# Turning the experts' activations: TensorE transposes replaced by a VectorE block transpose and ScalarE copies

## The chip, the core and the metric

The kernel runs on one core of a Trainium2 chip. A core has five engines that run in parallel, each through its own instructions in order: TensorE (PE, matrix products into PSUM), VectorE (DVE), ScalarE (ACT), GpSimd (POOL) and SyncE (SP). They wait for each other through semaphores. Data lie in SBUF, 128 partitions, and come from and go to device memory by DMA. The metric is the time of one execution on the device, in microseconds; lower is better.

## The reference

A layer norm feeds two branches whose results are added to the input: a gated linear recurrence with an output projection (`Wo`), and a mixture of 64 experts. The change is in the experts. Each takes up to 128 tokens of width 1024 and has a hidden width of 384:

```python
h = jax.nn.silu(jnp.einsum('ecd,efd->ecf', xg, w1)) * jnp.einsum('ecd,efd->ecf', xg, v1)
y = jnp.einsum('ecf,efd->ecd', h, w2)
yr = y[e_s, pos_c] * jnp.where(valid, w_s, 0.0)[:, None]
return jnp.zeros((T, D), x.dtype).at[tok_s].add(yr)
```

For the product with `w2`, TensorE sums over partitions, so the hidden features must lie on partitions. They come out of the first product with the tokens on partitions. So `h`, 128 tokens x 384 features, is turned once for each expert into three blocks of 128 features x 128 tokens. How this turn is made is what changes.

## The kernel before

Everything is fp32. The first part (attention, norm, routing, to about 1235 us in the profile) is not touched. The second part, `Experts.run`, treats the experts in a plan of groups: experts 0 and 1 alone, then 31 pairs (2, 3), (4, 5) and so on. Between the experts' products it places *steps* of the output projection of the other branch: 16 units of seven steps each, a step being four 128x512 matmuls of `steps` (L144, 8 rows in the profile, since each fp32 matmul makes two).

The order is written out by hand: inside `in_order`, TensorE, VectorE and ScalarE each keep the order of the program, so an instruction that waits holds all behind it on its engine. For a pair (e, e+1):

1. `hidden(e)` and `hidden(e+1)`: seven half products each (a Strassen-like scheme) into PSUM banks A, B, C, D (`hA` to `hD`), L977. ScalarE copies from the banks (L994 to L1001, L1007) and applies Silu (L1010). VectorE adds (L997 to L1009), turns the next expert's gathered tokens in blocks of 32x32 (`turned`, L920), and multiplies the two halves (L1012). `hidden(e)` also makes sums of the next expert's weights on VectorE (`right_sum`, L959; number 4, t4, is used by the last four matmuls of `hidden(e+1)`).
2. `turn_hidden(e)`: three TensorE transposes into bank D (L1021) and one ScalarE copy to `hT` (L1022).
3. One step of `project`, then `output(e)`: six matmuls with `w2` into banks D and T (L1030), each half scaled into `ys` by ScalarE (L1033), and a scatter with addition into the output from the POOL queue (L1034). There are two `ys` buffers, one for even and one for odd experts. VectorE makes sums for the next pair meanwhile.
4. `turn_hidden(e+1)`, two steps of `project`, `output(e+1)`; in every second pair one more step.

POOL's queue also holds the gathers of tokens (L871) and of token weights (L882), and the writes of the projection into the output (L1063); writes to the output follow each other. SP's queue holds the loads of the weights (L859) and of the projection's input (L1051).

Of the kernel before, what the change touches and what calls it, by code (L numbers as in the profile page):

```python
# [16 lines left out]
P = 128  # L17
B, S, D = 4, 1024, 1024
# [3 lines left out]
SH = S // 2  # L22
NM = SH // P
E, K, F, C = 64, 8, 384, 128
KF = F // P
TH = P // 2
Q = 32
NQ = P // Q
# [802 lines left out]
class Experts:  # L831
# [57 lines left out]
    def places(self):  # L889


        pools = self.pools
        t = pools.left.tile([P, NSLOT, KH, P], F32, tag="w", name="t23")
        t = t.rearrange("p a b c -> p (a b c)")
        u = pools.block("t4").rearrange("p a b -> p (a b)")
        n = KH * F
        self.t2, self.t3, self.t4 = (
            v.rearrange("p (k f) -> p k f", f=F) for v in (t[:, 0:n], t[:, n : 2 * n], u[:, 0:n])
        )
        self.p6, self.q = t[:, 2 * n : 2 * n + F], u[:, n : n + F]  # L900
        self.hT = self.p6.rearrange("p (j i) -> p j i", i=P)
        self.s = {0: pools.one.tile([P, 4, KH, TH], F32, tag="cur", name="s")}

    def more_places(self):
# [53 lines left out]
        }[n]  # L958
        self.nc.vector.tensor_tensor(to, a, b, ALU.subtract)  # L959

    def hidden(self, e, turn, then_next):

        nc = self.nc
        a11, a12, _, a22 = self.left_blocks(e)
        b11, b21, t1, b22 = self.right_blocks(e)
        s1, s2, s3, s4 = (self.s[e % 2][:, i] for i in range(4))
        ba, bb, bc, bd = (self.banks[n][:, 0:F] for n in "ABCD")  # L970
        lo, hi = slice(0, TH), slice(TH, P)

        def both(left, right):

            for k in range(len(left[3])):
                for half, (bank, a, b, ks) in ((lo, left), (hi, right)):
                    nc.tensor.matmul(  # L977
                        bank[half],
                        lhsT=a[:, ks[k], :],
                        rhs=b[:, ks[k], :],  # L980
                        start=(k == 0),
                        stop=(k == len(ks) - 1),
                        tile_position=(0, half.start),
                    )

        every, q, r, s, up = range(KH), self.q, self.acts[e % 2], self.p6, self.up
        both((bc, s3, self.t3, every), (bc, s4, b22, every))
        if then_next:  # L990
            for n in (3, 1):
                self.right_sum(e + 1, n)
        both((ba, a11, b11, every), (ba, s1, t1, every))
        nc.scalar.copy(q, ba)  # L994
        nc.scalar.copy(r[lo], ba[hi])
        nc.scalar.copy(r[hi], ba[lo])
        nc.vector.tensor_tensor(q, bc, q, ALU.add)  # L997
        nc.vector.tensor_tensor(up, q, r, ALU.add)
        both((bd, s2, self.t2, every), (bb, a12, b21, every))
        nc.scalar.copy(s[hi], bd[lo])  # L1000
        nc.scalar.copy(s[lo], bd[lo])  # L1001
        nc.vector.tensor_tensor(up, up, s, ALU.add)
        nc.vector.tensor_tensor(q[lo], q[lo], s[lo], ALU.add)
        if then_next:
            self.right_sum(e + 1, 2)
        both((bb, a22, self.t4, (0, 1)), (ba, a22, self.t4, (2, 3)))
        nc.scalar.copy(r[lo], ba[hi])  # L1007
        nc.vector.tensor_tensor(r, bb, r, ALU.add)
        nc.vector.tensor_tensor(r[lo], r[lo], q[lo], ALU.add)  # L1009
        nc.scalar.activation(r, r, AF.Silu)  # L1010
        self.turned(turn)
        nc.vector.tensor_tensor(r, r, up, ALU.mult)  # L1012
        if then_next:
            self.right_sum(e + 1, 4)
        for n in range(2):
            del self.weights[e, n]

    def turn_hidden(self, e):
        nc, pt = self.nc, self.banks["D"][:, 0:F].rearrange("p (j i) -> p j i", i=P)
        for j in range(KF):  # L1020
            nc.tensor.transpose(pt[:, j, :], self.acts[e % 2][:, j * P : (j + 1) * P], self.ident)  # L1021
        nc.scalar.copy(self.hT, pt)  # L1022

    def output(self, e):
        nc, ys, hT = self.nc, self.ys[e % 2], self.hT
        w2, wt = self.weights.pop((e, 2)), self.wt[:, e % NWT, e : e + 1]
        for h, cols in enumerate((H0, H1)):
            ps = self.banks["DT"[h]]
            for j in range(KF):
                nc.tensor.matmul(  # L1030
                    ps, lhsT=hT[:, j, :], rhs=w2[:, j, cols], start=(j == 0), stop=(j == KF - 1)
                )
            nc.scalar.mul(ys[:, cols], ps, wt)  # L1033
        nc.gpsimd.indirect_dma_start(  # L1034
            out=self.out,
            out_offset=bass.IndirectOffsetOnAxis(ap=self.idx[:, e : e + 1], axis=0),
            in_=ys,
            in_offset=None,
            compute_op=ALU.add,
        )  # L1040
        self.gather_wt(e + NWT)
# [54 lines left out]
    def run(self):  # L1096
        nc, pools, units = self.nc, self.pools, B * NM
        self.banks = {n: pools.bank(tag, [P, SH], f"h{n}") for n, tag in zip("ABCDT", "abcrt")}
        with in_order(self.tc, [mybir.EngineType.SP]):
            self.load(1, 1)  # L1100
            self.load_wo()
            self.load(0, 2)
            gated = self.load_gated(0)
            self.load(1, 0)
        for e in (1, 2):
            self.gather(e)
        wo_sums = right_sums(nc.vector, self.wo_b, lambda n: pools.block(f"wo_{n}"))

        plan = [((0,), 2, (1,), 0), ((1,), 1, (0,), 0)]
        plan += [((e, e + 1), 0, (1, 2), int(e % 4 == 0)) for e in range(2, E - 4, 2)]
        plan += [((e, e + 1), 0, (1, 1), 0) for e in (E - 4, E - 2)]
        todo, u, left = None, 0, 0

        def project(n):
            nonlocal todo, u, left, gated
            for _ in range(n):
                if left == 0:  # L1120
                    todo, left = self.project(u, gated), NSLOT
                next(todo, None)
                left -= 1
                if left == 0:
                    u += 1
                    gated = self.load_gated(u) if u < units else None

        with in_order(self.tc, ORDERED):
            for n in (2, 4):
                self.right_sum(0, n)  # L1130
            for _ in range(3):
                next(wo_sums)
            self.more_places()
            for g, (group, ahead, between, behind) in enumerate(plan):
                new = group[-1] + 1
                after = plan[g + 1][0] if g + 1 < len(plan) else ()
                for i, e in enumerate(group):
                    self.hidden(e, (*after[i : i + 1], E)[0], e != group[-1])
                    self.load(e + 2, 1)
                    if i == 0:  # L1140
                        self.load(e + 2, 0)
                    else:
                        self.load(e, 2)
                    if i == 0:
                        self.gather(new + 2)
                project(ahead)
                if g == 0:
                    for _ in wo_sums:
                        pass
                for i, e in enumerate(group):  # L1150
                    self.turn_hidden(e)
                    project(between[i])
                    if i == 0:
                        if len(after) > len(group):
                            self.turned(new + 1)
                        for n in after:
                            self.left_sums(n)
                        for n in (3, 1):
                            self.right_sum(new, n)
                    self.output(e)  # L1160
                    if i == 0 and len(group) > 1:
                        self.load(new + 1, 0)
                    if i == 0 and len(after) > 1:
                        self.gather(new + 3)
                    if e == group[-1]:
                        self.load(new, 2)
                        for n in (2, 4):
                            self.right_sum(new, n)
                project(behind)
            for _ in todo:  # L1170
                pass
# [48 lines left out]
```

## Time and profile before

| | |
|---|---|
| median of 3 runs | 2563.79 us (2562.29 to 2563.8) |
| the profiled execution | 2563.14 us, span 2561.4 us, granted TensorE clock 0.999 |
| POOL busy | 805.9 us, 31% |
| two stretches of 44 us among the pairs (1809 to 1853, 1853 to 1897 us) | TensorE busy 44.00 and 44.00, VectorE 29.30 and 29.59, ScalarE 12.73 and 10.99, POOL 19.26 and 15.55; DMA 0.94 and 0.91 busy |
| L1021 transposes 128x128 | 192, 273 ns each |
| L1022 copies 128x384 | 64, 475 ns each |
| L920 VectorE transposes 128x1024 | 64, 1229 ns each |

A row of the order of time has the start in us, the duration in us, the engine, the line, the operation, what it writes and reads, the shape, how many instructions are merged in it, and in brackets how long the engine sat idle before it and what ended that. Matmuls are pipelined: a row's duration is longer than the time after which the next one starts, so TensorE's pace is read from starts.

### The profile page before, as it was taken

The page shows a single profiled execution, that of the slowest core. Times are in us where ns is not written, and L with a number is a line of the kernel's source. Part 1 is how long each engine was busy: PE and PEld are TensorE (multiplying, and loading weights), DVE is VectorE, ACT ScalarE, POOL GpSimd, SP SyncE. Part 2 cuts the span into 40 slices and gives each one's busy share as a digit, 9 for nine tenths or more (in the row PEclk, how much of TensorE's full clock was granted, in tenths as well). Part 3 has the DMA queues.
Part 4 walks back from the last instruction along what each step waited for, and adds up shares of the span by engine and source line. Part 5 has one row for each costly group of instructions (what it writes and reads, how often), then busy time and mean ns, then how long its engine had stood idle before and what let it go on. Part 6 is the DMA issues. An engine that isn't in the chain of part 4 may idle for free.

```text
span 2561.4 us, 23153 instructions
## 1 busy us (share of the span) xinstructions
PE 2540.7 (99%) x8449; PEld 1124.8 (44%) x8449; DVE 1706.0 (67%) x2116; ACT 612.7 (24%) x1055; POOL 805.9 (31%) x631
## 2 busy tenths in 40 slices
PE   9999999999999999999999999999999999999998
PEld 5444444444444444444444444444444444444443
DVE  7956659474693747447776767667676767666673
ACT  3212212031111311112222222223232222223232
POOL 0453302101121110232353434344443434344421
PEclk9999999999999999999999999999999999999999
DMA  5755624543344532145898899989998899889995
GB/s 185 259 173 220 197 82 170 177 148 113 132 140 176 176 140 90 58 170 180 288 348 286 308 304 313 310 291 320 297 325 285 317 303 324 295 299 311 304 324 124
DMA packets 122497, 593.24 MB, mean 232 GB/s; under 512 B 15872, under 2 KB 52736, under 8 KB 89360
## 3 DMA queue, kind: packets, MB, share of 16 engines
q1 hardware_dynamic: 81488, 448.03, 47.7%
q0 software_dynamic: 40464, 143.72, 21.0%
q8 instruction: 67, 1.10, 0.2%
q14 instruction: 46, 0.38, 0.0%
q10 hardware_dynamic: 432, 0.01, 0.0%
HBM read 483.67 MB, written 124.81 MB: 238 GB/s over the span
## 4 chain that ended last, share of the span: by engine, by line
PE 90%; DVE 8%; issue 1%; DMA 1%; ACT 0%; SPq 0%; POOL 0%; POOLq 0%; DVEq 0%; ACTq 0%
PE pa_g L144 8%; PE pa_o L144 8%; PE hC L977 7%; PE hA L977 7%; PE hD L1030 6%; PE hT L1030 6%; PE hD L977 6%; PE pa_q L144 6%; PE pa_v L144 5%; PE pc_g L144 4%; PE pc_o L144 4%; PE pc_q L144 3%; PE hB L977 3%; PE pc_v L144 3%; DVE cur L555 2%; PE pb_o L144 2%
## 5 line engine op out<-in xcount | busy, mean ns | idle before, releaser
L871 POOL DMA_INDIRECT xg<-rows,tables x256 | 307.9, 1203 | 303.4 <-DVE xgT L920 234.8
L959 DVE TENSOR_TENSOR t<-w 128x1536 f32<-128x1536 f32 x128 | 224.1, 1751 | 261.9 <-PE hC L977 259.1
L1034 POOL DMA_INDIRECT out_dram<-ys,tables x64 | 132.9, 2077 | 394.6 <-ACT ys L1033 202.2
L144 PE MATMUL pa_g<-xT,w 128*128 128x512 f32 x512 | 230.8, 594 | 0.0
L144 PE MATMUL pa_v<-xT,w 128*128 128x512 f32 x480 | 216.8, 593 | 2.5 <-ACT sc_v L155 2.5
L144 PE MATMUL pa_q<-xT,w 128*128 128x512 f32 x480 | 216.6, 593 | 1.2 <-ACT sc_q L155 1.2
L977 PE MATMUL hC<-t,s 128*64 128x384 f32 x512 | 177.3, 489 | 0.0
L977 PE MATMUL hC<-w,s 128*64 128x384 f32 x512 | 177.3, 489 | 0.0
L1030 PE MATMUL hD<-w,t 128*128 128x512 f32 x384 | 175.3, 592 | 0.6 <-ACT t L1022 0.6
L977 PE MATMUL hA<-w,s 128*64 128x384 f32 x512 | 175.6, 486 | 0.0
L977 PE MATMUL hD<-t,s 128*64 128x384 f32 x512 | 175.6, 486 | 0.0
L977 PE MATMUL hB<-w,xgT 128*64 128x384 f32 x512 | 175.6, 486 | 0.0
L977 PE MATMUL hA<-w,xgT 128*64 128x384 f32 x512 | 175.6, 486 | 0.0
L1030 PE MATMUL hT<-w,t 128*128 128x512 f32 x384 | 175.2, 592 | 0.0
L144 PE MATMUL pa_o<-wo_T,gated 128*128 128x512 f32 x384 | 172.7, 592 | 0.0
L144 PEld LDWEIGHTS pa_g<-xT,w 128*128 128x128 f32 x512 | 96.4, 190 | 122.9 <-issue 122.1
L701 POOL DMA_DIRECT2D gated<-y x64 | 48.1, 757 | 303.0 <-DVE y L696 288.6
L144 PEld LDWEIGHTS pa_q<-xT,w 128*128 128x128 f32 x480 | 90.9, 190 | 116.6 <-issue 112.7
L144 PEld LDWEIGHTS pa_v<-xT,w 128*128 128x128 f32 x480 | 90.2, 190 | 114.8 <-issue 109.6
L144 PE MATMUL pc_v<-xT,w 128*128 128x512 f32 x256 | 115.4, 593 | 2.2 <-ACT sc_v L155 2.2
L144 PE MATMUL pc_q<-xT,w 128*128 128x512 f32 x256 | 115.4, 593 | 2.1 <-ACT sc_q L155 2.1
L144 PE MATMUL pc_g<-xT,w 128*128 128x512 f32 x256 | 115.5, 594 | 0.0
(243 smaller groups left out, 4309.1 us busy)
## 6 DMA issues: line engine op xcount, KB each, us to landing
w<-in_w_dram SPq DMA_DIRECT2D x128, 1536.0 KB, 9.5
w<-in_v_dram SPq DMA_DIRECT2D x64, 1536.0 KB, 8.7
w<-wsum SPq DMA_DIRECT2D x36, 1792.0 KB, 7.5
wsum<-w POOLq DMA_DIRECT2D x12, 1792.0 KB, 6.1
x<-in_x_dram SPq DMA_DIRECT2D x32, 512.0 KB, 9.3
rows<-x POOLq DMA_DIRECT2D x32, 512.0 KB, 4.6
gated<-y POOLq DMA_DIRECT2D x64, 256.0 KB, 4.7
gated<-gated SPq DMA_DIRECT2D x16, 1024.0 KB, 6.5
```

What stands on the lines that cost most here:

```text
L144: nc.tensor.matmul(ps, lhsT=lhs[:, slot, k, :], rhs=blocks[right][:, k, :], start=start and k == 0, stop=stop and k == KH - 1, skip_group_ ...
L555: nc.vector.match_replace(cur, eight, cur, 0.0)
L701: nc.gpsimd.dma_start(out=gated[b, :, :, slot, m, :].rearrange("u p j -> p u j"), in_=yc[:, h * SH : (h + 1) * SH].rearrange("p (u j) -> p ...
L871: nc.gpsimd.indirect_dma_start(out=self.xg[:, e % 2 * NQ + r, :], out_offset=None, in_=self.rows.rearrange("n (q c) -> (n q) c", q=NQ), in ...
L959: self.nc.vector.tensor_tensor(to, a, b, ALU.subtract)
L977: nc.tensor.matmul(bank[half], lhsT=a[:, ks[k], :], rhs=b[:, ks[k], :], start=(k == 0), stop=(k == len(ks) - 1), tile_position=(0, half.st ...
L1030: nc.tensor.matmul(ps, lhsT=hT[:, j, :], rhs=w2[:, j, cols], start=(j == 0), stop=(j == KF - 1))
L1034: nc.gpsimd.indirect_dma_start(out=self.out, out_offset=bass.IndirectOffsetOnAxis(ap=self.idx[:, e : e + 1], axis=0), in_=ys, in_offset=No ...
```

## The change

The TensorE transposes, their copy and the tile `hT` in the place of t2/t3 go. In their place `split_hidden(e)`, at the end of `hidden(e)`, has VectorE turn the activations in blocks of 32x32 into the left half of `ys`; after it every block is turned, but lies on the partitions of its tokens. `turn_hidden(e)` then makes 16 ScalarE copies, each of three blocks (32 partitions x 3 x 32), from partition quarter r to quarter q, into the right half of `ys`, where `output` reads them.

The place of the turn moves too. In a pair the first expert's copies are issued inside the second's `hidden`, after the copies from bank D (L1001); the second's after the first step of `project`. The plan is rewritten so that each pair has one step ahead of the first output and the rest ahead of the second, as before; the single experts have two steps ahead of the output (before: three around the transposes for expert 0, one for expert 1).

```diff
-        self.hT = self.p6.rearrange("p (j i) -> p j i", i=P)
...
-    def hidden(self, e, turn, then_next):
+    def hidden(self, e, turn, then_next, last=None):
...
         nc.scalar.copy(s[hi], bd[lo])
         nc.scalar.copy(s[lo], bd[lo])
+        if last is not None:
+            self.turn_hidden(last)
...
         nc.vector.tensor_tensor(r, r, up, ALU.mult)
+        self.split_hidden(e)
         if then_next:
             self.right_sum(e + 1, 4)
...
+    def split_hidden(self, e):
+
+        t = self.ys[e % 2][:, 0:F]
+        self.nc.vector.transpose(
+            t.rearrange("p (x i) -> p x i", i=Q), self.acts[e % 2].rearrange("p (x j) -> p x j", j=Q)
+        )
+
     def turn_hidden(self, e):
-        nc, pt = self.nc, self.banks["D"][:, 0:F].rearrange("p (j i) -> p j i", i=P)
-        for j in range(KF):
-            nc.tensor.transpose(pt[:, j, :], self.acts[e % 2][:, j * P : (j + 1) * P], self.ident)
-        nc.scalar.copy(self.hT, pt)
+
+        split = self.ys[e % 2][:, 0:F].rearrange("p (j q i) -> p j q i", q=NQ, i=Q)
+        for r in range(NQ):
+            for q in range(NQ):
+                self.nc.scalar.copy(
+                    self.hT(e)[q * Q : (q + 1) * Q, :, r * Q : (r + 1) * Q],
+                    split[r * Q : (r + 1) * Q, :, q, :],
+                )
+
+    def hT(self, e):
+
+        return self.ys[e % 2][:, SH : SH + F].rearrange("p (j i) -> p j i", i=P)
...
-        plan = [((0,), 2, (1,), 0), ((1,), 1, (0,), 0)]
-        plan += [((e, e + 1), 0, (1, 2), int(e % 4 == 0)) for e in range(2, E - 4, 2)]
-        plan += [((e, e + 1), 0, (1, 1), 0) for e in (E - 4, E - 2)]
+        plan = [((e,), 2, 0, 0) for e in range(2)]
+        plan += [((e, e + 1), 1, 2, int(e % 4 == 0)) for e in range(2, E - 4, 2)]
+        plan += [((e, e + 1), 1, 1, 0) for e in (E - 4, E - 2)]
...
-                project(ahead)
+                project(1)
+                self.turn_hidden(group[-1])
+                project(ahead - 1)
...
                 for i, e in enumerate(group):
-                    self.turn_hidden(e)
-                    project(between[i])
...
+                    else:
+                        project(between)
                     self.output(e)
```

## The prediction

> **What bounds the kernel now.** I read the busy times, then the list of what TensorE waited for, then the order of time of each engine in the experts' stage.
>
> ```profile
> PE 2540.7 (99%) x8449; PEld 1124.8 (44%) x8449; DVE 1706.0 (67%) x2116; ACT 612.7 (24%) x1055; POOL 805.9 (31%) x631
> PE 90%; DVE 8%; issue 1%; DMA 1%; ACT 0%; SPq 0%; POOL 0%; POOLq 0%; DVEq 0%; ACTq 0%
> PE hD L1030 <- ACT t L1022: 0.6, 1, 0.6
> ```
>
> The first line says that TensorE is busy 99% of the span and ScalarE 24%; the second, that the chain that ended last is TensorE's; the third is the only wait of TensorE after 1200 us, 0.6 us. So the experts' stage is TensorE in one unbroken row. Work taken off it shortens the kernel; any hole made in it lengthens it. Now the joint between two experts of a pair and what follows, on TensorE and on ScalarE:
>
> ```profile
> 1827.11 0.49 PE L977 MATMUL hA<-t,xgT 128*64 128x384 f32 x1
> 1827.53 0.55 PE L1021 MATMUL hD<-ident,act 128*128 128x128 f32 x3
> 1827.91 3.60 PE L144 MATMUL pa_o<-wo_B,gated 128*128 128x512 f32 x8
> 1831.35 2.74 PE L1030 MATMUL hD<-w,t 128*128 128x512 f32 x6
> 1833.92 2.74 PE L1030 MATMUL hT<-w,t 128*128 128x512 f32 x6
> 1836.50 0.49 PE L1021 MATMUL hD<-ident,act 128*128 128x128 f32 x3
> 1836.83 3.60 PE L144 MATMUL pb_o<-wo_B,gated 128*128 128x512 f32 x8
> ...
> 1824.28 0.48 ACT L995 COPY act<-hA 64x384 f32<-64x384 f32 x1
> 1824.77 0.47 ACT L996 COPY act<-hA 64x384 f32<-64x384 f32 x1
> 1826.39 0.47 ACT L1000 COPY t<-hD 64x384 f32<-64x384 f32 x1 [1.15 <-PE hB L977]
> 1826.89 0.47 ACT L1001 COPY t<-hD 64x384 f32<-64x384 f32 x1
> 1827.65 0.48 ACT L1007 COPY act<-hA 64x384 f32<-64x384 f32 x1 [0.28 <-PE hA L977]
> 1829.60 0.52 ACT L1010 ACTIVATE act<-act 128x384 f32<-128x384 f32 x1 [1.48 <-DVE act L1009]
> ```
>
> Starts give the pitches: a step of `project` (8 rows) takes 3.44 us, an `output` (12 rows) 5.15, a `hidden` 9.03 (rows of hC begin 9.03 apart in the two experts). Call T0 the end of the pair's second `hidden`: 1827.11 + 0.32 = 1827.43.
>
> **Removed.** The first expert's transposes hold TensorE from T0 to 1827.91, 0.48 us (0.10 of it the wait for bank D, which L1001 empties), the second's 0.33 (1836.50 to 1836.83): 0.81 us a pair, 31 pairs, 25.1 us. Of the two single experts, the first gives 0.33 and the second 1.18 (its transposes start at 1267.13, its output at 1268.31: here L1022 was waited for); 1.5 together. L1022 (475 ns) goes too, and hides anyway.
>
> **Added on VectorE: one 128x384 transpose an expert.** L920 is 128x1024 in 1229 ns, L451 128x512 in 679; 1.07 ns a column gives 0.54 us. In a pair's first expert it stands ahead of `right_sum(e+1, 4)`, which began 0.44 us after L1012 and now begins 0.57 us later: ready at 1825.94 for a matmul at 1826.14. L673 to L606 shows 0.15 us from VectorE to TensorE, so it arrives 0.05 before. Bounds 0 and 0.1 us a pair (3 us); I take 0. The new wait, for the scatter of ys two experts back, is a rival below.
>
> **Added on ScalarE: 16 copies of 32x96 an expert.** No row shows a 32-partition copy. The nearest SBUF-to-SBUF rows are L465 (128x1024, 1044 ns), less 928 elements at 0.83 ns = 274 ns, and L394 (128x8, 209 ns) plus 88 elements = 282 ns; partitions don't matter, since L995 on 64 takes 476 ns and L994 on 128 takes 479. So 275 ns. What decides is how closely they follow each other. ScalarE has two habits in this trace. Copies that keep their partitions overlap: two 128x512 copies at L155 start 0.47 us apart and last 0.57. Copies that change the partition at which they read or write do not: L995 to L996 0.49 at 0.48, L1000 to L1001 0.50 at 0.47, and the four of L669 start 0.57 to 0.59 apart at 0.58. Every one of the 16 writes another quarter than the one before it. I take 0.275 + 0.015 = 0.29 us.
>
> Here the Trainium skill speaks twice. ScalarE: Activation LUTs (What ACT_TABLE_LOAD costs) gives 186 ns + 0.833 ns an element, 266 ns here, and an overlap of about 93 ns back to back: 0.173 us each, and the change would win. VectorE: DVE Perf Modes (Two Vector instructions with no wait between them) says that an instruction whose start quarter differs from the last one's is held until all earlier ones have finished. It is stated for VectorE, but the ScalarE rows above behave so, and I go by the rows. The same ScalarE page's budget (Rules for kernel authors), 0.3 us and 0.83 ns an element, would be 0.38; that is for a bias read through a pointer, which a copy hasn't.
>
> **What this does to a pair.** The first expert's copies are queued between L1001 and L1007, from 1827.38 (T0 - 0.05). They end at T0 - 0.05 + 15 x 0.29 + 0.275 = T0 + 4.58; ScalarE to TensorE is 0.17 (L1001 ends 1827.36, the transposes start 1827.53), so its output can start at T0 + 4.75. TensorE has one step of `project` to do and is there at T0 + 3.44. **Stall 1.30 us, saving 0.81, net +0.49 a pair; 31 pairs, 15.2 us.**
>
> Behind those copies wait L1007 and all after it: it starts at T0 + 4.59 instead of 0.22; the two sums (0.51 and 0.58 on), L920 (0.47) and the product (1.16) come to T0 + 7.31, the split ends at 8.4, its 16 copies at 13.1, the first scaling of ys at 13.8, the second at 14.4. TensorE is at the second output at 4.75 + 5.15 + 6.87 = 16.8: nothing late, 3.7 us spare. The last two pairs put one step there instead of two, 13.3, and bank D is free at 13.8 + 0.17: 0.65 each, 1.3. VectorE's sums for the next pair, which end 4 to 8 us before its first matmul now (1804.99 of 1809.32, 1844.67 of 1852.3), still end 2 to 4 us ahead of it (T0 + 19.7 of 21.9, or 21.6 of 25.3).
>
> A single expert has all on one line: L1007 at T0 + 0.22, product 2.94, split to 4.0, copies from 4.13 (behind `project`'s own copy) to 8.75, output at 8.92 where TensorE stands ready after two steps at 6.88: 2.04 each, 4.1, less the 1.5 removed: +2.6.
>
> SP issues the same loads in the same order; those that follow an output come 0.5 to 0.7 us later against T0, with some 10 us between landing (9.5 us) and first use. POOL's order is the same too; the scatter of the first expert leaves some 4 us later.
>
> **Sum:** 15.2 + 1.3 + 2.6 = +19 us on the profiled execution, 2563.14 (span 2561.4), so 2582; the median shown is 0.65 higher: **2583**. 0.2% (5 us) is what this measurement can tell from no change.
>
> **Rivals.**
>
> *The copies overlap* (the other side). At 0.18 us each the first expert's are done at T0 - 0.05 + 2.7 + 0.275 + 0.17 = 3.1, ahead of TensorE at 3.44: no stall in any pair, 25.1 won, single experts 0.4 x 2 - 1.5. 2563.8 - 26 = 2538. It decides as soon as a copy's pitch is under 0.21; net zero in a pair is at 0.26. For it: L155, L305, and 128x2 rows at L424 that start 0.19 us ahead of the next. Against it: every change of quarter in the trace. 0.14.
>
> *The copies are dearer.* At 0.38 + 0.02 the stall is 3.06, net 2.25 a pair, 70 us; the single experts (3.8 each) and last pairs (2.4 each) add 11: 2645. For it only the budget named above; against it the rows L465 and L394. 0.07.
>
> *The scatter is late.* The split waits until ys of two experts back has been added into the output. In every second pair (one after steps 4 to 6) POOL sends the first scatter at T0 + 14.5, then the two projected halves (9.4 us on, as at 1798.05 and 1807.48), then the second scatter 14 us after those (1807.48 to 1821.62): T0 + 38, landed at 47 (9.0 median, 13.8 at most). The next pair's second split wants it at 47.8. If it lands late, VectorE and ScalarE wait, and TensorE does once it is over 3.7 us late. All at 13.8: 0.3 us in 15 pairs. All three landings late together: some 10 us, 6 x 15 = 90. I take none; 0.09 that it costs over 5 us, 2590 to 2615.
>
> *As forecast* 0.63, its own range 2569 to 2595 (pitch 0.27 to 0.31, and t4's 3 us). Some 0.07 lies near no change, a pitch of 0.25 to 0.265.
>
> The range leaves out the overlap (0.14) and the dear copies: 2564 to 2613. Faster 0.14, same 0.07, slower 0.79.
>
> **What will show it.** Copies at some 275 ns, starting 0.29 apart; no L1021 rows; a wait of TensorE at the first output of each pair for ScalarE, about 1.2 us 31 times, and about 2 us twice; none at the second outputs but for the last two pairs; TensorE's busy share down to some 97%. Starts 0.18 apart, or a DMA as releaser of the split and then of TensorE, would prove me wrong.

## The result, and the profile after

The changed kernel takes 2616.87 us (median of five runs, 2614.03 to 2621.89) against 2563.04: 1.0212 times the time before, 95% interval 1.0200 to 1.0223. The forecast was 2583, range 2564 to 2613. The sign was right, the size was not: +54 us instead of +19. The profiled execution took 2617.79 us, 54.65 more than that of before.

First the busy times of the page:

```profile
PE 2543.6 (97%) x8257; PEld 1104.6 (42%) x8257; DVE 1741.3 (67%) x2180; ACT 852.0 (33%) x2015; POOL 770.3 (29%) x631
```

Then TensorE's waits in the experts' stage (line, what it waited for, us in all, times, longest of them):

```profile
PE pa_o L144 <- DVE gated L55: 24.1, 14, 6.1
PE hD L1048 <- ACT ys L1033: 20.4, 33, 1.6
PE hD L1048 <- ACT ys L1051: 7.7, 13, 5.8
```

There was one wait of 0.6 us before. The second row is the one that was forecast: `output` (now L1048) waits for the copies (L1033). The first was not: a projection step waits for VectorE's sums of its input (L55), 14 times, once for 6.1 us. The third is the second output's wait for ScalarE's scalings of the first output (L1051). Idle time is counted from modelled ends, so the account below is made from starts.

The forecast joint, in the order of time of TensorE and ScalarE:

```profile
1890.51 3.70 PE L144 MATMUL pa_o<-wo_T,gated 128*128 128x512 f32 x8
1894.77 2.84 PE L1048 MATMUL hD<-w,ys 128*128 128x512 f32 x6 [0.56 <-ACT ys L1033]
...
1889.87 0.47 ACT L1001 COPY t<-hD 64x384 f32<-64x384 f32 x1
1890.24 4.47 ACT L1033 COPY ys<-ys 32x96 f32<-32x96 f32 x16
1894.74 0.47 ACT L1009 COPY act<-hA 64x384 f32<-64x384 f32 x1
```

The 16 copies take 4.47 us, and the output starts 0.06 us after the last ends. From step to output are 4.26 us where 3.44 to 3.54 were free of waits.

The joint that was not forecast, in a pair that comes after steps 4 to 6: POOL, VectorE, TensorE, ScalarE. (L1052 is the scatter of `ys`, L1081 the projected halves, L1014 the product.)

```profile
1819.56 2.69 POOL L1052 DMA_INDIRECT out_dram<-ys,tables  x1 [1.91 <-ACT ys L1051]
1830.11 0.96 POOL L1081 DMA_DIRECT2D out_dram<-olo  x1 [6.23 <-issue]
1830.75 1.25 POOL L1081 DMA_DIRECT2D out_dram<-ohi  x1
1845.50 1.63 POOL L1052 DMA_INDIRECT out_dram<-ys,tables  x1 [13.50 <-ACT t L1001]
...
1852.20 0.51 DVE L1014 TENSOR_TENSOR act<-act,up 128x384 f32<-128x384 f32 x1
1857.67 0.58 DVE L1024 STREAM_TRANSPOSE ys<-act 128x384 f32<-128x384 f32 x1 [4.96 <-DMA out_dram<-ys,tables]
1858.85 0.69 DVE L55 TENSOR_TENSOR gated<-gated 128x512 f32<-128x512 f32 x1
...
1854.74 3.60 PE L144 MATMUL pb_o<-wo_B,gated 128*128 128x512 f32 x8
1859.69 3.67 PE L144 MATMUL pa_o<-wo_T,gated 128*128 128x512 f32 x8 [1.35 <-DVE gated L55]
1863.52 2.84 PE L1048 MATMUL hD<-w,ys 128*128 128x512 f32 x6 [0.15 <-ACT ys L1051]
...
1858.28 4.47 ACT L1033 COPY ys<-ys 32x96 f32<-32x96 f32 x16 [5.95 <-DVE ys L1024]
1862.78 0.69 ACT L1051 ACTIVATE ys<-hD,act 128x512 f32<-128x512 f32 x1
```

The product is done at 1852.71, but the split (L1024) writes into `ys`, out of which a scatter issued at 1845.50 is still reading; it lands 12.1 us later and the split starts at 1857.67. The releasers in brackets on POOL's rows are not the true ones: the first scatter landed at 1829.6 and the second half at 1844.6, and each time the next write to the output was issued 0.5 to 0.9 us later.

TensorE then waits twice. Behind the split VectorE has the sums L54 to L57, and the second step waits for L55. After that step the second output waits for bank D, which holds half of the first output until its scaling (L1051) has read it; that scaling stands on ScalarE behind the 16 copies, and they behind the split. The scaling ends at 1863.47 and the output starts at 1863.52. From the split to this scaling ScalarE has no pause and waits for nothing else, so by the trace TensorE would have lost the same 1.9 us here without L55: the wait that ends last is that for bank D. This is so in 12 of the 14 pairs that waited for L55, with 0.05 us from scaling to output in each.

The split waited in 15 of 64 experts, 80.2 us in all: the second expert of every second pair.

And the granted clock, in two stretches around the longest such wait (busy times of TensorE, its weight loads, VectorE, ScalarE and POOL; then the clock, the DMA share and GB/s):

```profile
2110.00:2117.00 7.00, 4.14 (x10) 1.52 (x8) 0.00 (x0) 0.00 (x0) 5.48 (x6) 1.00 0.91 265
2117.00:2124.00 7.00, 3.72 (x5) 1.69 (x6) 5.61 (x12) 4.94 (x18) 3.98 (x5) 0.54 0.61 217
```

TensorE waits from about 2114.0 to 2120.28, and its clock is halved from 2117.6 for 6.83 us, the first of the work after the wait included. Before, the mean clock was 0.999; here it is 0.996, with three such stretches in the experts' stage (3.41, 6.83 and 6.83 us). In the two pairs among the 14 that have one, the second step runs so long that the output starts 1.4 and 1.7 us later than bank D would have let it.

The account, from the starts of TensorE's rows in the experts' stage, in us against the profiled execution of before:

| part | us |
|---|---|
| transposes gone (22.3 in 63 experts, 1.2 in one) | -23.5 |
| first outputs wait for copies: 31 x 0.82 | +25.4 |
| single experts: 2 x 1.77 | +3.5 |
| late split, 14 pairs: the two steps ahead of the second output, with its wait for bank D; 3.1 of it half clock | +35.0 |
| late split, last pair but one: second output (L1051) | +5.9 |
| outputs: first matmul 0.10 slower after a wait; 2.6 of it half clock | +7.4 |
| sum, of 54.65 | +53.7 |

### The profile page after: what moved, and what is told of

The parts are those of the page before. It is cut to its first block, busy times and chain, and to the rows that moved or that the text cites. A ratio compares the mean times of both kernels' runs of the same rounds, so it can differ in the third digit from the quotient of the medians.

```text
span 2616.0 us, 23821 instructions
## 1 busy us (share of the span) xinstructions
PE 2543.6 (97%) x8257; PEld 1104.6 (42%) x8257; DVE 1741.3 (67%) x2180; ACT 852.0 (33%) x2015; POOL 770.3 (29%) x631
## 5 line engine op out<-in xcount | busy, mean ns | idle before, releaser
L871 POOL DMA_INDIRECT xg<-rows,tables x256 | 275.5, 1076 | 351.7 <-DVE xgT L919 274.3
L1033 ACT COPY ys<-ys 32x96 f32<-32x96 f32 x1024 | 274.9, 268 | 131.1 <-DVE ys L1024 119.9
L1052 POOL DMA_INDIRECT out_dram<-ys,tables x64 | 138.1, 2158 | 414.7 <-ACT ys L1051 134.0
L1048 PE MATMUL hD<-w,ys 128*128 128x512 f32 x384 | 182.7, 612 | 28.1 <-ACT ys L1033 20.4
L144 PE MATMUL pa_o<-wo_T,gated 128*128 128x512 f32 x384 | 179.2, 610 | 24.1 <-DVE gated L55 24.1
L1048 PE MATMUL hT<-w,ys 128*128 128x512 f32 x384 | 175.2, 592 | 0.0
L1048 PEld LDWEIGHTS hD<-w,ys 128*128 128x128 f32 x384 | 69.9, 192 | 137.3 <-issue 70.5
L144 PEld LDWEIGHTS pa_o<-wo_T,gated 128*128 128x128 f32 x384 | 71.8, 193 | 124.9 <-issue 124.9
```

The source lines that it names most:

```text
L144: nc.tensor.matmul(ps, lhsT=lhs[:, slot, k, :], rhs=blocks[right][:, k, :], start=start and k == 0, stop=stop and k == KH - 1, skip_group_ ...
L871: nc.gpsimd.indirect_dma_start(out=self.xg[:, e % 2 * NQ + r, :], out_offset=None, in_=self.rows.rearrange("n (q c) -> (n q) c", q=NQ), in ...
L1033: self.nc.scalar.copy(self.hT(e)[q * Q : (q + 1) * Q, :, r * Q : (r + 1) * Q], split[r * Q : (r + 1) * Q, :, q, :],)
L1048: nc.tensor.matmul(ps, lhsT=hT[:, j, :], rhs=w2[:, j, cols], start=(j == 0), stop=(j == KF - 1))
L1052: nc.gpsimd.indirect_dma_start(out=self.out, out_offset=bass.IndirectOffsetOnAxis(ap=self.idx[:, e : e + 1], axis=0), in_=ys, in_offset=No ...
```

## The experiments

Theory S: the excess is the odd experts' split, held by the scatter out of `ys`. Theory C: it is the copies on ScalarE, and the scatter only stands beside them. Later runs ask why the scatter is late, and what the copies' pitch comes from.

**own.** Odd experts split into the place of `q` and turn into that of `s`, both dead at that point.

```diff
-        t = self.ys[e % 2][:, 0:F]
+        t = self.q if e % 2 else self.ys[0][:, 0:F]
...
-        return self.ys[e % 2][:, SH : SH + F].rearrange("p (j i) -> p j i", i=P)
+        t = self.p6 if e % 2 else self.ys[0][:, SH : SH + F]
+        return t.rearrange("p (j i) -> p j i", i=P)
```

> The changed kernel, but odd experts split into the place of q and turn into the place of s (p6), not into ys, so no split of an odd expert waits for a scatter. Theory S (the excess over the forecast is the odd experts' split held by the scatter out of ys): 2563.0 less 23.5 for the transposes, plus 31 x 0.82 for the first outputs, 3.7 for the single experts and 3.3 for slower first matmuls after a wait: 2572 (2568 to 2577), granted clock back at 0.999, no wait on L55. Theory C (the copies on ScalarE are the cause, and the scatter only stands beside them): 2600 to 2617.

Measured: 2574.53 us (2573.02 to 2574.78), 1.0040 times before (1.0026 to 1.0054); clock 0.999. Of 53.8 us, 42.3 are gone. No wait on L55 is left; TensorE's largest in the experts' stage is the forecast one:

```profile
PE hD L1050 <- ACT ys L1034: 18.9, 32, 1.6
```

Theory S stands, theory C falls. By the same account from starts, -23.5 + 25.4 + 3.5, with 3.5 for slower first matmuls and 1.4 in the last pair but one, is 10.3; measured 10.9.

**split_only.** The kernel before, transposes kept, with the split into `ys` added behind L1012.

```diff
         nc.vector.tensor_tensor(r, r, up, ALU.mult)
+        nc.vector.transpose(
+            self.ys[e % 2][:, 0:F].rearrange("p (x i) -> p x i", i=Q),
+            r.rearrange("p (x j) -> p x j", j=Q),
+        )
```

> The kernel before with its TensorE transposes, and the VectorE split into ys added to it, its result unused, so that it does nothing but hold VectorE and wait for the scatter. If that wait alone made the loss (a rival to S, which needs the scatter of the first expert 4 us later and the chain behind the copies): 2580 to 2600. By S the split would wait some 2 to 3 us in every second pair and TensorE would not notice: 2563 to 2566.

Measured: 2564.78 us, 1.0004 times before (0.9995 to 1.0013): no difference. The view of the split's line shows that it did wait:

```profile
L1013 DVE STREAM_TRANSPOSE ys<-act x64: 578/578/579, 1241.1 to 2528.7; 128x384 f32<-128x384 f32 x64
...
  DMA out_dram<-ys,tables: 50.0, 15
```

15 waits of 3.3 us on average cost nothing, because here VectorE wants the split some 4 us earlier: L1007 is not queued behind 16 copies. So the wait alone is not the loss. It takes the wait and the later chain together.

**early.** The changed kernel, first expert's copies ahead of those from bank D instead of behind them.

```diff
         nc.scalar.copy(r[hi], ba[lo])
+        if last is not None:
+            self.turn_hidden(last)
...
         nc.scalar.copy(s[lo], bd[lo])
-        if last is not None:
-            self.turn_hidden(last)
```

> The changed kernel, but the first expert's copies are issued ahead of the copies from bank D (after L996) instead of behind them. Both theories: the first outputs' wait (0.82 us and 0.1 of slow start, 31 times) goes, 28 us; the scatter waits stay. 2589 (2582 to 2595). If the first outputs wait for something other than the place in ScalarE's queue: 2617 as before.

Measured: 2634.66 us (2628.01 to 2641.45), 1.0268 times before: slower than the changed kernel by 18, where 28 us less was expected. This was a miss of both theories. The first outputs' wait is gone, as expected (the step ahead of them takes 3.54 us, not 4.26). But TensorE is now earlier at each pair, while the row of additions into the output takes as long as before (39.2 us on average from the issue of the first scatter to the landing of the second, against 38.4), so the splits wait longer (104.5 us for 80.2) and TensorE with them. L55 is waited for 51.0 us in all. One such place in TensorE's order of time:

```profile
1867.37 3.60 PE L144 MATMUL pb_o<-wo_B,gated 128*128 128x512 f32 x8
1874.33 6.68 PE L144 MATMUL pa_o<-wo_T,gated 128*128 128x512 f32 x8 [3.37 <-DVE gated L55]
```

and the stretch around it, with the granted clock ahead of the DMA share:

```profile
1873.00:1880.00 7.00, 5.67 (x7) 2.50 (x8) 6.83 (x13) 5.48 (x18) 3.17 (x3) 0.54 0.58 220
```

After the wait the eight rows take 6.68 us instead of 3.60. The mean clock fell to 0.984, with a halved stretch at 14 of 15 such waits (holes of 2.5 to 7.3 us, from starts). A wait of 3.4 us costs itself and up to another 3. So the longer waits ate the gain, and the half clock made the loss: by starts these 14 pairs lose 50 us more than in the changed kernel, 27 of it longer waits, and 23 of it the second output starting later than bank D would have let it.

**own_early.** The edits of *own* and *early* together.

> Both edits together. Theory S: no wait of TensorE left in a pair; 2563.0 less 23.5 plus 3.7 for the single experts: 2543 (2540 to 2548), faster than both kernels. Theory C: 2570 to 2590.

Measured: 2549.04 us (2548.4 to 2549.75), 0.9944 times before (0.9927 to 0.9960): faster than both kernels. It is 6 above the expectation: the step behind `hidden` takes 3.54 us, not 3.44, 31 times (3 us), and the last pair but one waits 1.6 us for a load of weights. In one account: -23.5 for the transposes, 5.1 for these two with 0.3 us in the last pair, 3.5 for the single experts, 0.3 in the outputs: -14.6; measured -14.55.

**scale_first** and **early_scale_first.** `ys` stays the place, but in a pair the second expert's copies come behind the scalings of the first expert's output; without and with the early copies.

```diff
                 project(1)
-                self.turn_hidden(group[-1])
+                if len(group) == 1:
+                    self.turn_hidden(group[-1])
...
                     else:
+                        self.turn_hidden(e)
                         project(between)
```

> The changed kernel with ys still the place of split and turn, but in a pair the second expert's copies are issued behind the two scalings of the first expert's output instead of ahead of them. So the first expert's scatter leaves some 4 us earlier against TensorE, and the row of additions into the output (scatter, two projected halves, scatter) ends 4 us earlier. Theory S (that row decides): the odd experts' splits wait some 1 to 2 us instead of 5.3, TensorE no longer waits on L55, the clock stays at 0.999: 2575 (2571 to 2580). If the splits are held by something else on the DMA side, such as the loads of weights: 2600 to 2617.

Measured: 2578.95 us (2577.88 to 2580.38), 1.0060 times before. The splits waited 16.1 us in all, 9 times, and TensorE's waits on L55 fell to 2.8 us. The order of the copies and the scalings on ScalarE is worth 38 of the 54 us: what made the scatter late was that the scalings ahead of the first scatter stood behind the second expert's copies.

> The same, with the first expert's copies ahead of the copies from bank D as well. TensorE is then 0.9 us earlier at each pair, 1.8 us against the row of additions, so the splits wait 3 to 4 us. Theory S with TensorE's slack of about 3 us: near 2551, at most 2565, against 2634.7 with the early copies alone. If the slack is smaller: 2575 to 2600.

Measured: 2557.75 us, 0.9980 times before (0.9972 to 0.9988), with runs from 2552.38 to 2567.8. The splits waited 29.3 us, 13 times, 2.3 each, and TensorE three times, 5.5 us. The same edit that cost 18 us in *early* wins 21 here. The spread of runs, 15 us against 4 for the kernel before, is what one expects where DMA landings lie within a microsecond or two of the point from which TensorE waits; that is argued, not shown.

**thirds.** *own_early* with each copy cut in three that read and write the same quarters.

```diff
-                self.nc.scalar.copy(
-                    self.hT(e)[q * Q : (q + 1) * Q, :, r * Q : (r + 1) * Q],
-                    split[r * Q : (r + 1) * Q, :, q, :],
-                )
+                for j in range(KF):
+                    self.nc.scalar.copy(
+                        self.hT(e)[q * Q : (q + 1) * Q, j, r * Q : (r + 1) * Q],
+                        split[r * Q : (r + 1) * Q, j, q, :],
+                    )
```

> The kernel with places of its own and early copies (2549), but each copy of 32x96 cut into three of 32x32 that read and write the same quarters, so that two of three follow a copy of the same quarters. If a change of quarter is what keeps copies from overlapping: starts some 0.12 to 0.14 us apart inside three and 0.22 to 0.23 between threes, 16 x 0.48 = 7.7 us an expert. If ScalarE never overlaps copies on 32 partitions: 0.22 throughout, 10.6 us. If the copies overlapped in the changed kernel as well: 0.12 throughout, 5.8 us. The time is longer than 2549 by what the longer rows of copies do to the outputs: 2600 to 2680.

Measured: 2690.97 us in a single execution, 11 over the range written for it; the longer row of copies holds up the outputs and brings the half clock back (0.985). The starts answer the question. A copy of 212 ns is followed after 0.117 to 0.125 us by one with the same quarters and after 0.220 to 0.225 by one with others; 48 of them:

```profile
1851.60 7.41 ACT L1035 COPY t<-t 32x32 f32<-32x32 f32 x48 [1.68 <-DVE t L1024]
```

The row takes 7.41 us, where 7.7 was written for a hold at each change of quarter. So ScalarE overlaps copies of 32 partitions as well as of 128, and here a change of quarter is what forbids it. That source and target of a copy share the tile `ys` is not the reason: in *own* the odd experts' copies go from one tile to another and start 0.28 us apart as well.

## Why the prediction was wrong

**Right.** What bounds the kernel, and that a hole in TensorE's row costs its length. The order on ScalarE and its effect: L1009 behind the copies, the first output late, second outputs of ordinary pairs not. The copies: forecast 275 ns at 0.29 us, measured 268 ns at 0.280. The choice between the row and the rule was right: by the estimate from the overlap in the Trainium skill's ScalarE: Activation LUTs (What ACT_TABLE_LOAD costs) the copies would have been 0.173 us apart. That overlap of about 93 ns is there in *thirds* (212 ns less 117 to 125), but only between copies of the same quarters; the rule of VectorE: DVE Perf Modes (Two Vector instructions with no wait between them) that an instruction of another quarter is held, written for VectorE, describes ScalarE here. The sign was not luck: without the wait for the scatter, *own* is slower too, and its 2574.53 lies in the 2569 to 2595 given for *as forecast*.

**Right in mechanism, off in size.** First outputs: forecast 1.30 us, measured 0.82, plus 0.10 for a slower first matmul. The pitch took 0.15 off, the first copy followed L1001's start after 0.37 us instead of 0.49, and the start of TensorE behind the last copy took 0.06 instead of 0.17; the other 0.10 is the time from the end of `hidden` to the step's start, which the sum did not count for TensorE. Transposes: 25.1 + 1.5 was forecast, 23.5 went, since 0.10 of the first expert's 0.48 is not a wait for bank D but the passage from `hidden` to wider matmuls, which stays. Single experts: 2.04 forecast, 1.77 measured. Without the scatter (*own*) the kernel is 11 us slower, where these steps had said 19.

**Wrong: the rival of the late scatter, put at 0.09 with no cost taken.** It measured 41 us, 35.0 + 5.9 in the account. Its chain was worked out in full, and three of its terms were too short. In us from the start of the first step of a pair, at 1805.40:

| | forecast | measured |
|---|---|---|
| first scatter issued | 14.5 | 14.2 |
| to the first projected half | 9.4 | 10.5 |
| from there to the second scatter | 14 | 15.4 |
| its landing | 9.0 | 12.1 |
| landed | 47 | 52.2 |
| wanted by the split | 47.8 | 47.3 |

The largest of the three is the landing, and the trace of before had it. The sum used the median over all 64 scatters; this scatter, by its own place in the pair, is another case. In the kernel before, the view of the scatter's line for the one at 1821.62 alone ends:

```profile
DMA to landing us min/median/max: 11.9/11.9/11.9
```

The 15 of that place landed after 11.4 to 13.8 us, the others mostly after 8 to 11. With 12 the forecast would have had the split some 2 us late in every second pair, still within the cover; the two intervals, taken from a trace in which the row of additions began 4 us earlier in the pair, added 2.5. Of the signs that the prediction named for its being wrong, a DMA as releaser of the split and then of TensorE is the one that came.

**Wrong: the cover, taken as 3.7 us.** The path was right: a late split makes the second expert's copies late, and the second output with them. But 3.7 is the time from the end of the copies (13.1) to the output (16.8). The output also needs bank D, free at 13.8 + 0.17 by the same forecast, which leaves 2.8; the prediction counted bank D in the last two pairs only. In the pair shown the split was 4.96 us late and the second output 1.91, so the cover was 3.05, and it was 3.0 to 3.1 in all 12 pairs at full clock. A demand that comes sooner was overlooked: L55 stands behind the split in VectorE's queue and held the second step for 1.5 us in that pair, a cover of 3.4. That is the longer of the two, so at full clock it adds nothing; where the wait brings the half clock, the second step decides.

**Not thought of: the clock.** Of the 54 us about 6 are TensorE at half clock after its own waits: 3.1 in the two pairs above and 2.6 in the second output of the last pair but one (7.93 us for 5.35).

## What to carry to other kernels

A buffer that is read by a DMA on its way out is not free scratch. Before something new writes there, take the landing of that very transfer at its place in the loop, not the median of its kind, and look on every engine at what is queued behind the instruction that will wait.

Where two rows run beside each other, here TensorE's and the row of additions into the output, speeding up only the first makes it wait for the second: the same edit lost 18 us or won 21, by whether the second row had slack. Where it had none, the longer waits took back the gain and the half clock after them made the loss.

Moving data across quarters of the partitions on ScalarE cost the full duration of each copy here (268 ns, 280 apart), with no overlap, so it is worth it only where those copies can be laid into the engine's idle time and off the path that it feeds.

## What was not expected of the hardware

Short waits bring the half clock, and where a wait falls decides. The Trainium skill (TensorE: Matmul & The Clock Gate, Part 1) has the clock halved after an idle window of about 3.4 us which runs freely. In the changed kernel and in *early* the stretches at half clock during the experts' stage are 3.41, 6.83 or 10.24 us long, one, two or three such windows, and in each trace they begin whole multiples of 3.413 us apart, which agrees. But the window need not be idle from end to end: holes in TensorE's row of 2.5 and 2.7 us were already followed by one (*early* at 1787.58 and 1613.50), while one of 2.9 us (*early* at 2048.45) was not, and none of 2.0 us or less was.

*thirds* shows what decides. In each of its 31 pairs the first output comes after a hole of the same 2.65 us, and 18 of these were followed by the half clock and 13 not, as in these two pairs, one after the other (4.54 us for six rows at half clock, 2.84 at full; the wait in brackets counts from modelled ends):

```profile
1847.25 4.54 PE L1051 MATMUL hD<-w,ys 128*128 128x512 f32 x6 [2.48 <-ACT t L1003]
1890.70 2.84 PE L1051 MATMUL hD<-w,ys 128*128 128x512 f32 x6 [2.48 <-ACT t L1003]
```

Laid on the grid of 3.413 us, the 18 have 1.98 us or more of the hole within one window and the 13 have 1.87 or less. The hole in *early* at 2048.45 lies across two windows, with 2.1 us in one, so the border is not the same to a tenth in every trace. A wait of 2.5 us may thus cost more than itself, or may not, by where it happens to fall.
